# Turning every row of attention weights through DRAM, with fewer VectorE steps a row, in a two-layer graph network

## The chip, the cores and the metric

The kernel runs on one core of a Trainium2 chip. The time is the device time of one execution in microseconds (us): 2100.51 is the median of 3 runs, 2095.24 to 2102.91. The engines of the core run their own instruction queues in the order in which they were written: TensorE (PE) multiplies matrices, VectorE (DVE) and ScalarE (ACT) work on SBUF and PSUM, GpSimd (POOL) does small arithmetic, and SyncE (SP) issues nearly all DMA transfers.

## The reference, cut to what matters

There are N = 3327 nodes with 256 features each; `adj` is 3327 x 3327, sparse, with weights on its edges and on its diagonal.

```python
h = relu(layernorm(x))
# layer 0, two steps n = 0, 1, from Xf = Xa = h
R = adj + eye;  R = R / R.sum(-1)                       # row-normalised
  probs = softmax((Xa @ W1.T @ W2.T) @ (Xa @ W3.T).T)   # 3327 x 3327
  A = probs kept down from the largest until 0.9 of the sum is passed, then renormalised
  Xf = R @ Xf;  Xa = A @ Xa
  Z += Xf @ U1[n].T + Xa @ U2[n].T
x = x + layernorm(h + Z) * g + b
# layer 1, four heads of 64 on h = relu(layernorm(x))
hp = h @ W;  s = hp . a_src;  d = hp . a_dst
attn = softmax over j with adj[i, j] > 0 of leaky_relu(s_i + d_j)
x = x + elu(attn @ hp)
```

## The kernel before

All data are float32. The 3327 nodes make 26 tiles of 128 (`NT`); the last has 127.

**Layer 0** has two kinds of work. A *row* (class `Row`, one for each step and each tile i of 128 query nodes) is the whole search for the attention weights of those queries. PE computes logits in two halves (`logits`), ACT writes their exponentials into an SBUF buffer `e` of 128 x 3328 (`exps`; one row in five uses a buffer called `qq`), ACT counts and sums against trial thresholds (`count`), POOL steps the threshold (`step`, `before`), DVE picks out the largest values below it (`window`, `sort`), decides the exact cut (`choose`), and clears what lies below it (`drop`). Ties at the cut are resolved by position: the 3327 columns are cut into pieces, and each piece gets its own threshold, `thr`. The weights then have to be turned, since PE contracts over partitions. Columns 0 to 3071 are turned in three groups g of 1024 (`turn_blocks`, `put_blocks`, `get_blocks`): DVE transposes 32 x 32 blocks in place, SP writes the group to `blocks` in DRAM and reads it back with four DMAs (o = 0 to 3). Columns 3072 to 3327 are turned by PE itself (`turn`: two transposes into a PSUM tile `px`, then a copy by ACT or DVE into `et`). `BLOCKED` says which rows go this way: all 26 of step 0, the first 23 of step 1; the last three rows of step 1 are turned by PE in all 26 tiles. `attend_blocks` and `attend` multiply with `rhs`, into the PSUM bank `acca`. `finish1` and `finish2` then project a row's result; in `finish2`, `stage` and `scale` write layer 1's operand `main`.

A *full* (class `Full`, one for each step and tile t) is a block row of R @ Xf: seven loads of `adj` transposed into tiles `at` (four buffers, four j each), and 26 matmuls into the PSUM bank `accf`. The identity in R is put in afterwards: for step 0 in `take` or `add`, and in `own`, which adds c times the reciprocal sum to what is stored in `ys`.

**Layer 1** (`attend_neighbours`) goes over four blocks b of 832 query nodes, each with 26 tiles j of neighbours. SP loads adjacency tiles, ACT makes a 0/1 mask (`mask`), DVE makes the masked exponentials of four heads (`exponents`, four instructions a tile), and PE does `product` (eight matmuls, both halves c of 416 columns) and `sums` (eight, for the denominators). Sums are done for two tiles at a time (`JG = 2`). After the 26 tiles of a block `leave` copies the PSUM banks out, and `turn`, `quotient`, `parts`, `add_x1`, `join`, `store` finish seven tiles of up to 128 rows.

**The order of the work** is written by a planner (class `Plan`): every piece is given an engine, a length, a rank, the pieces that it needs, the buffers that it takes and gives back, and a lag until others see its end. The planner runs through them once and issues, on each engine, the ready piece of the lowest rank. What it writes is fixed: on the chip an engine waits at the head of its queue even if later work is ready. So a figure in the plan (a lag, a rank) moves instructions on every queue. A row's attention has rank 30n + i, its logits 2.5 less; the fulls of step 0 have min(1 + 1.15t, 27). They are what PE does when no row is ready.

Of the kernel before, what the change touches and what calls it, by code (L numbers as in the profile page):

```python
# [10 lines left out]
F32 = mybir.dt.float32  # L11
# [8 lines left out]
P = 128  # L20
# [29 lines left out]
BLOCKED = (NT, NT - 3)  # L50
# [421 lines left out]
class Plan:  # L472
# [3 lines left out]
    LAG = {"PE": 0.2, "ACT": 0.2, "DVE": 0.15, "POOL": 0.1, "SP": 2.2}  # L476
# [23 lines left out]
    def either(self, first, second, rank, *args, **kw):  # L500

        p = self.put(*first[:2], rank, first[2], *args, **kw)
        p["on"] = {e: (length, fn, self.LAG[e], 0.0) for e, length, fn in (first, second)}
        p["engine"] = ""
        return p
# [82 lines left out]
def fast(  # L588
# [58 lines left out]
    with ExitStack() as l0:  # L647
# [23 lines left out]
        blocks = spill.tile([3, 4, P, 2 * P], F32, name="blocks")  # L671
# [27 lines left out]
        def weights():  # L699
# [39 lines left out]
            a = plan.put("PE", 0.25, -200.0, turn, take=["px"], needs=[plan.put("SP", 0.02, -201.0, lambda: None, lag=8.0)])  # L739
# [126 lines left out]
        plan = Plan(dict(rows=1, mvs=3, pl=2, px=2, acca=1, accf=1, et=3, at=4, y=1, e2=3, mask=2, e5=1, qg=2, **BUFS))  # L866
# [4 lines left out]
        class Row:  # L871
# [3 lines left out]
                "b w t0 t1 t2 u g k2 p0 p1 p2 p3 D0 D1 D2 v z r0 s0 s1 s2 h x th tq mid dh kh fl d up h0 h1 room zs cnt "  # L875
# [38 lines left out]
            def exps(self, k):  # L914
                pl = self.pl.pop(k)
                to = self.e[:, PART * k : PART * k + pl.shape[1]]
                if k < 3 and self.i < BLOCKED[self.n]:
                    to = to.rearrange("p (g q t) -> p g t q", g=4, t=2)
                    pl = pl.rearrange("p (g t q) -> p g t q", g=4, t=2)
                S.activation(  # L920
                    to,
                    pl,
                    AF.Exp,
                    accum_out=(self.p0, self.p1, self.p2, self.p3)[k],
                )

            def row_sum(self):
                k = self.NAMES.index("p0")
                S.activation(self.sc[:, k + 4 : k + 8], self.sc[:, k : k + 4], AF.Copy, accum_out=self.s)
# [114 lines left out]
            def choose(self):  # L1044
# [14 lines left out]
                V.scalar_tensor_tensor(out_, win, nxt, keep, ALU.is_gt, ALU.mult, accum_out=self.cnt)  # L1059
                V.tensor_sub(self.m, met[:, 2, i], self.cnt)  # L1060
                ties = small.tile([P, PIECES * 8], F32, name="rest", bufs=1).rearrange("p (c r) -> p c r", r=8)
                V.tensor_scalar(ties, self.cands, nxt, None, ALU.is_equal)
                num, upto = (small.tile([P, 4], F32, name=name, bufs=1) for name in ("num", "upto"))
                V.tensor_reduce(num[:, :3], ties[:, :15, :].rearrange("p (a c) r -> p a (c r)", a=3), AX.X, ALU.add)
                V.tensor_reduce(num[:, 3:], ties[:, 15, :], AX.X, ALU.add)
                V.tensor_tensor_scan(upto, num, num, 0.0, ALU.add, ALU.bypass)
                V.scalar_tensor_tensor(num, upto, self.m, num, ALU.is_le, ALU.mult, accum_out=met[:, 4, i])
                self.thr = small.tile([P, 4], F32, name="thr")
                V.tensor_scalar(upto, upto, self.m, 2.0**-24, ALU.is_gt, ALU.mult)
                V.tensor_scalar(self.thr, upto, 1.0 - 2.0**-24, nxt, ALU.add, ALU.mult)  # L1070

            def drop(self, o):

                piece = self.e[:, o * PART : min((o + 1) * PART, N)]
                V.scalar_tensor_tensor(piece, piece, self.thr[:, o : o + 1], piece, ALU.is_gt, ALU.mult)  # L1075
# [6 lines left out]
            def turn(self, g):  # L1082
                m = min(4, NT - 4 * g)
                pt = self.pt[g] = ps_x.tile([P, 4, P], F32, name="px")
                for k in range(m):
                    j = 4 * g + k
                    T.transpose(pt[:, k, :], self.e[:, j * P : (j + 1) * P], ident)

            def turned_by_s(self, g):
                self.turned(g, S.copy)  # L1090

            def turned_by_v(self, g):
                self.turned(g, V.tensor_copy)

            def turned(self, g, copy):
                m = min(4, NT - 4 * g)
                self.et[g] = etpool.tile([P, 4, P], F32, name="et")
                copy(self.et[g][:, :m, :], self.pt.pop(g)[:, :m, :])

            def attend(self, g):  # L1100
                if g == 0:
                    self.acc = ps_a.tile([P, D], F32, name="acca")
                et = self.et.pop(g)
                for j in range(4 * g, min(4 * g + 4, NT)):
                    T.matmul(
                        self.acc, et[:, j - 4 * g, :], rhs[self.n][:, j, :], start=(j == 0),
                        stop=j == NT - 1 and self.i >= BLOCKED[self.n],
                    )
# [28 lines left out]
        class Full:  # L1137
# [41 lines left out]
            def add(self):  # L1179
                rs = rsum[:, self.t : self.t + 1]  # L1180
                f, here = self.f[:, :D], c[:, self.t, :]
                if not self.added:
                    V.tensor_add(f, f, self.src[:, self.t, :D])
# [934 lines left out]
```

## Time and profile before

| what | before |
|---|---|
| median of 3 runs | 2100.51 us |
| the profiled execution: its own time, its span | 2100.08 us, 2098.2 us |
| mean granted TensorE clock | 0.994 |
| layer 0 (start to 1619 us): PE, DVE, ACT, POOL busy | 1570.2, 1292.8, 1043.0, 979.6 us |
| layer 1 (1619 to 2083 us): PE, DVE, ACT busy | 463.9, 429.6, 251.2 us |
| DMA in layer 0 and layer 1 | 173 and 125 GB/s |

The profiled execution lies 0.4 us below the median. A busy time is the time in which at least one instruction of the engine was under way; matmuls overlap each other, so their mean durations are longer than the pace at which they follow one another. In the groups of PE one float32 matmul shows as two records, and a transpose as one.

### The profile page before, as it was taken

The page shows a single profiled execution, that of the slowest core. Times are in us where ns is not written, and L with a number is a line of the kernel's source. Part 1 is how long each engine was busy: PE and PEld are TensorE (multiplying, and loading weights), DVE is VectorE, ACT ScalarE, POOL GpSimd, SP SyncE. Part 2 cuts the span into 40 slices and gives each one's busy share as a digit, 9 for nine tenths or more (in the row PEclk, how much of TensorE's full clock was granted, in tenths as well). Part 3 has the DMA queues.
Part 4 walks back from the last instruction along what each step waited for, and adds up shares of the span by engine and source line. Part 5 has one row for each costly group of instructions (what it writes and reads, how often), then busy time and mean ns, then how long its engine had stood idle before and what let it go on. Part 6 is the DMA issues. An engine that isn't in the chain of part 4 may idle for free. (4 is left out here: it accounts for less than half of the span.)

```text
span 2098.2 us, 34334 instructions
## 1 busy us (share of the span) xinstructions
PE 2037.8 (97%) x10695; PEld 1415.2 (67%) x10695; DVE 1729.7 (82%) x4105; ACT 1300.0 (62%) x2480; POOL 990.7 (47%) x2170
## 2 busy tenths in 40 slices
PE   8999999999999989989999999999999999999997
PEld 6477777878787778767878787787877333333332
DVE  5689897778876871578998979988987999999895
ACT  5767665666556621777778776778652547465552
POOL 4476654446544630567778777777772000000001
PEclk9999999999999999999999999999999999999999
DMA  4188888678877685697787888887743544453341
GB/s 116 45 190 186 194 180 195 168 152 196 189 183 172 176 186 138 199 232 165 181 189 176 203 188 191 185 191 192 182 126 89 157 141 142 125 147 115 112 127 34
DMA packets 580513, 338.56 MB, mean 161 GB/s; under 512 B 327931, under 2 KB 533281, under 8 KB 580321
## 3 DMA queue, kind: packets, MB, share of 16 engines
q1 hardware_dynamic: 579424, 336.06, 66.4%
q8 instruction: 87, 1.43, 0.3%
q14 instruction: 106, 0.86, 0.1%
q10 hardware_dynamic: 896, 0.21, 0.0%
HBM read 242.86 MB, written 93.05 MB: 160 GB/s over the span
## 5 line engine op out<-in xcount | busy, mean ns | idle before, releaser
L959 ACT ACTIVATE junk<-e,sc 128x3327 fp8e5<-128x3327 f32 x147 | 451.0, 3068 | 31.4 <-POOL sc L996 29.8
L1128 PE MATMUL acca<-rhs,e 128*128 128x256 f32 x1872 | 426.8, 381 | 4.6 <-DMA e<-blocks 4.6
L1128 PEld LDWEIGHTS acca<-rhs,e 128*128 128x128 f32 x1872 | 364.9, 197 | 48.7 <-issue 6.0
L1153 PE MATMUL accf<-c,at 128*128 128x256 f32 x1352 | 316.5, 385 | 17.1 <-DMA at<-in_adjt_dram 8.5
L1153 PE MATMUL accf<-main,at 128*128 128x257 f32 x1352 | 313.3, 381 | 5.4 <-ACT main L1304 2.5
L1153 PEld LDWEIGHTS accf<-c,at 128*128 128x128 f32 x1352 | 252.8, 192 | 67.5 <-DMA at<-in_adjt_dram 10.2
L1153 PEld LDWEIGHTS accf<-main,at 128*128 128x128 f32 x1352 | 250.4, 190 | 54.3 <-issue 11.5
L1022 DVE MAX8 cands<-y 128x8 f32<-128x205 f32 (+1 forms) x832 | 242.9, 361 | 3.6
L1918 POOL TENSOR_TENSOR qq<-qq 128x256 f32<-128x256 f32 x4 | 3.0, 759 | 457.0 <-ACT qq L1914 457.0
L1017 DVE SCALAR_TENSOR_TENSOR y<-e,sc 128x1639 f32<-128x1639 f32 x84 | 165.1, 1965 | 62.9 <-POOL sc L1007 61.7
L920 ACT ACTIVATE e<-pl 128x1024 f32<-128x1024 f32 (+1 forms) x168 | 152.9, 920 | 75.4 <-PE pl L905 74.7
L1752 ACT ACTIVATE et<-at 128x448 bf16<-128x448 f32 (+1 forms) x204 | 112.6, 552 | 128.6 <-DVE e L1763 73.3
L1779 PE MATMUL pl<-e,main 128*64 128x416 f32 x1024 | 190.4, 517 | 0.1
L1075 DVE SCALAR_TENSOR_TENSOR e<-e,thr 128x1024 f32<-128x1024 f32 (+1 forms) x168 | 178.4, 1066 | 2.4 <-DMA at<-in_adjt_dram 0.3
L905 PE MATMUL pl<-kt,qg 64*128 64x512 f32 (+1 forms) x832 | 173.7, 536 | 0.4 <-ACT qq L920 0.4
L1112 DVE STREAM_TRANSPOSE e<-e 128x1024 f32<-128x1024 f32 x117 | 146.1, 1248 | 3.7
L1779 PEld LDWEIGHTS pl<-e,main 128*64 128x64 f32 x1024 | 70.3, 137 | 111.0 <-issue 91.5
L1763 DVE SCALAR_TENSOR_TENSOR e<-c,low,et 128x832 f32<-128x832 f32 x128 | 128.8, 1070 | 6.1 <-issue 3.2
L905 PEld LDWEIGHTS pl<-kt,qg 64*128 64x128 f32 x832 | 71.5, 186 | 83.4 <-issue 76.2
L1751 ACT ACTIVATE at<-at 128x448 f32<-128x448 f32 (+1 forms) x204 | 110.8, 543 | 25.7 <-DMA at<-in_adjt_dram 25.6
L1763 DVE SCALAR_TENSOR_TENSOR e<-qq,low,et 128x832 f32<-128x832 f32 x120 | 120.5, 1073 | 4.1 <-PE accf L1793 2.9
L959 ACT ACTIVATE junk<-qq,sc 128x3327 fp8e5<-128x3327 f32 x35 | 107.4, 3068 | 10.7 <-POOL sc L996 10.4
(550 smaller groups left out, 3540.7 us busy)
## 6 DMA issues: line engine op xcount, KB each, us to landing
at<-in_adjt_dram SPq DMA_DIRECT2D x414, 256.0 KB
blocks<-e SPq DMA_DIRECT2D x117, 512.0 KB
e<-blocks SPq DMA_DIRECT2D x468, 128.0 KB
at<-in_adjt_dram SPq DMA_DIRECT2D x102, 192.0 KB
blocks<-qq SPq DMA_DIRECT2D x30, 512.0 KB
qq<-blocks SPq DMA_DIRECT2D x120, 128.0 KB
at<-in_adjt_dram SPq DMA_DIRECT2D x52, 128.0 KB
ys<-ystage SPq DMA_DIRECT2D x26, 256.0 KB
```

Of the source, the lines that this page charges most:

```text
L905: T.matmul(pl[:, lo : lo + m], qg[self.n, self.i // 4][half, self.i % 4, :], kt[half, 512 * k : 512 * k + m], start=True, stop=True,)
L920: S.activation(to, pl, AF.Exp, accum_out=(self.p0, self.p1, self.p2, self.p3)[k],)
L959: S.activation(junk[:, :N], self.e[:, :N], fn, bias=t, scale=-1.0, accum_out=dst, saturate=False)
L1017: V.scalar_tensor_tensor(self.y[:, : hi - lo], self.e[:, lo:hi], self.up, self.e[:, lo:hi], ALU.is_lt, ALU.mult, accum_out=(self.h0, self. ...
L1022: V.max(self.cands[:, a * PIECES // 2 + k, :], self.y[:, at[k] - lo : at[k + 1] - lo])
L1075: V.scalar_tensor_tensor(piece, piece, self.thr[:, o : o + 1], piece, ALU.is_gt, ALU.mult)
L1112: V.transpose(part, part)
L1128: T.matmul(self.acc, lhs, rhs[self.n][:, j, :], start=(j == 0), stop=stop and j == js[-1])
L1153: T.matmul(self.acc[:, : self.w], self.at[j // JC][:, j % JC, :], self.src[:, j, : self.w], start=(j == 0), stop=(j == NT - 1),)
L1752: S.activation(to, src, AF.Sign)
L1763: V.scalar_tensor_tensor(held["e"][:, k, :], extra["both"][b % 2][:, k, :], low[:, j, k : k + 1], held["mask"], ALU.max, ALU.mult,)
L1779: T.matmul(q["acc"][a][k * FH : (k + 1) * FH, c, :C], main[:, j, h * FH : (h + 1) * FH], held["e"][:, h, c * C : (c + 1) * C], start=(j == 0),
```

## The change

It has eight parts, and the plan is made anew with all of them.

1. All rows are turned through DRAM, in all 26 tiles. `BLOCKED`, `turn`, `turned`, `attend` go. The third group now has 1280 columns: `blocks` holds 13 slices, its DVE transpose, its put and its four gets are a quarter larger.
2. `drop` has three pieces in place of four (1024, 1024, 1279 columns). `choose` finds the ties with one scan over the 128 candidates.
3. `exps` writes the last 255 columns with two instructions, of 128 and 127, into the order that the blocks want.
4. The identity is added by POOL into the diagonal tile of `at` (`diagonal`), once for each full. The additions in `take`, `add` and `own` go. PE's matmul of that tile needs the addition.
5. `stage` in `finish2` makes layer 1's operand on ACT from PSUM, with four instructions scaled by `qd`; DVE's `scale` goes.
6. In the last block of layer 1 the last six tiles (`LATE = 6`) are multiplied by halves: first half c = 0 of all six, then half c = 1. `leave_half` copies the first half out while the second is multiplied.
7. The exponentials of the first two tiles of layer 1 get rank 54.2, before the last rows of layer 0; the four `e` buffers, `c` and `rhs` are handed to layer 1 in another order (`ec`).
8. In the plan: lags of 8 in place of 6 for puts, 4 in place of 3.3 for `at` loads, 7 in place of 3 for the store to `ys`; the fulls of step 0 have rank 2 + 1.3t; empty pieces no longer take a slot of SP or POOL.

```diff
-BLOCKED = (NT, NT - 3)
-        blocks = spill.tile([3, 4, P, 2 * P], F32, name="blocks")
+        blocks = spill.tile([NT // 2, P, 2 * P], F32, name="blocks")
...
             def exps(self, k):
...
+                if k < 3:
+                    S.activation(to, pl.rearrange("p (g t q) -> p g t q", g=4, t=2), AF.Exp, accum_out=sums[k])
+                else:
+                    S.activation(to[:, 0, 0, :], pl[:, :P], AF.Exp, accum_out=self.p3)
+                    S.activation(to[:, 0, 1, : m - P], pl[:, P:], AF.Exp, accum_out=self.p4)
...
             def choose(self):
...
-                V.tensor_scalar(ties, self.cands, nxt, None, ALU.is_equal)
-                num, upto = (small.tile([P, 4], F32, name=name, bufs=1) for name in ("num", "upto"))
-                V.tensor_reduce(num[:, :3], ties[:, :15, :].rearrange("p (a c) r -> p a (c r)", a=3), AX.X, ALU.add)
-                V.tensor_reduce(num[:, 3:], ties[:, 15, :], AX.X, ALU.add)
-                V.tensor_tensor_scan(upto, num, num, 0.0, ALU.add, ALU.bypass)
-                V.scalar_tensor_tensor(num, upto, self.m, num, ALU.is_le, ALU.mult, accum_out=met[:, 4, i])
+                V.tensor_scalar(ties, self.cands.rearrange("p c r -> p (c r)"), nxt, None, ALU.is_equal)
+                V.tensor_tensor_scan(ties, ties, ties, 0.0, ALU.add, ALU.bypass)
+                self.thr = small.tile([P, PIECES], F32, name="thr")
+                V.tensor_scalar(self.thr, ties[:, 7::8], self.m, 2.0**-24, ALU.is_gt, ALU.mult)
+                V.tensor_scalar(self.thr, self.thr, 1.0 - 2.0**-24, nxt, ALU.add, ALU.mult)
+                ends = ties[:, 39:80:40]
+                V.scalar_tensor_tensor(ends, ends, self.m, ends, ALU.is_equal, ALU.mult, accum_out=met[:, 4, i])
...
+            def part(self, g):
+                return self.e[:, g * PART : (g + 1) * PART if g < 2 else NP]
...
+            def diagonal(self):
+                own = self.at[self.t // JC][:, self.t % JC, :]
+                GP.tensor_add(own, own, ident)
...
-                V.scalar_tensor_tensor(y, c[:, t, :], rsum[:, t : t + 1], y, ALU.mult, ALU.add)
-            y = plan.put("SP", 0.5, r + 0.3, store, needs=[a], give=["ystage"], lag=3.0)
+            y = plan.put("SP", 0.5, r + 0.3, store, needs=[a], give=["ystage"], lag=7.0)
...
+                for k in range(H):
+                    part = slice(k * FH, (k + 1) * FH)
+                    S.activation(main[:, t, part], pm[:, part], AF.Copy, scale=qd[:, t, k : k + 1])
...
-            if row.i < BLOCKED[row.n]:
...
-                last = plan.put("PE", 0.22, rank - 0.01, row.turn, 6, needs=[drops[3]], take=["px"])
...
+                b = plan.put("SP", 0.5, rank - 1.0, row.put_blocks, g, needs=[b], lag=8.0)
...
-                plan.put("SP", 0.4, rank, f.load, q, needs=[after], take=["at"], lag=3.3) for q in range(-(-NT // JC))
+                plan.put("SP", 0.4, rank, f.load, q, needs=[after], take=["at"], lag=4.0) for q in range(-(-NT // JC))
...
+            a, own = None, plan.put("POOL", 0.4, -90.0, f.diagonal, needs=[loads[t // JC]])
...
+                    if b == 3 and j >= NT - LATE:
+                        for c in range(2):
+                            r = rank if c == 0 else r0 + 9.0
+                            p_ = plan.put("PE", 0.71, r, product, 0, (c,), needs=[x_, last_acc, halves[c]])
+                            p_ = plan.put("PE", 0.71, r, product, 1, (c,), needs=[x_, y_, p_])
+                            halves[c] = plan.put(
+                                "PE", 0.76, r, sums, (c,), needs=[p_, last_den], give=[mine] if c else []
+                            )
+                        continue
...
+                def leave_half(c, q=q):
...
+                    for k in range(2):
+                        S.copy(q["ot"][k][:, c * C : (c + 1) * C], q["acc"][k][:, c, :C])
+                    S.copy(q["ot"][2][:, c * C : (c + 1) * C], q["den"][c][:, :C])
...
-                full(n, t, (min(1.0 + 1.15 * t, 27.0) if n == 0 else base + 1.0 + t), [p[0] for p in sources], [p[1] for p in sources] if n == 0 else loaded[0])
+                full(n, t, (2.0 + 1.3 * t if n == 0 else base + 1.0 + t), [p[0] for p in sources], [p[1] for p in sources] if n == 0 else loaded[0])
```

In the lists of instructions of the two kernels PE has 176 fewer (all transposes), DVE 337 fewer, ACT 98 more, POOL 52 more and SP 45 more; every matmul of before is still there.

## The prediction

> **What bounds the kernel now.** I read first the busy times of the page, then the same by stage, because a share over the whole span mixes two layers with different limits.
>
> ```profile
> PE 2037.8 (97%) x10695; PEld 1415.2 (67%) x10695; DVE 1729.7 (82%) x4105; ACT 1300.0 (62%) x2480; POOL 990.7 (47%) x2170
> 0.00:1619.00 1619.00, 1570.17 (x7283) 1243.54 (x7283) 1292.77 (x3596) 1042.96 (x1868) 979.59 (x2157) 0.99 0.74 173
> 1619.00:2083.00 464.00, 463.91 (x3392) 169.52 (x3391) 429.59 (x488) 251.16 (x597) 5.53 (x6) 1.00 0.43 125
> 2083.00:2098.00 15.00, 3.73 (x25) 2.18 (x21) 7.37 (x21) 5.92 (x16) 5.59 (x7) 0.72 0.20 64
> ```
>
> The columns of the last three lines are the stretch, its length, the busy time of PE, PE's weight loads, DVE, ACT and POOL, the granted clock, the DMA share and GB/s. In layer 0 PE is idle for 1619.0 - 1570.2 = 48.8 us, in layer 1 for none, and after it comes a tail of 15 us. So the time is PE's work, plus 48.8, plus the tail. DVE, at 1292.8 of 1619, has no claim of its own except through latency.
>
> A busy PE need not be at its best pace, so next I read how closely its instructions follow one another, in the order of time.
>
> ```profile
> 1567.91 1.04 PE L1087 MATMUL px<-ident,e 128*128 128x128 f32 x8
> 1568.78 1.89 PE L1105 MATMUL acca<-rhs,et 128*128 128x256 f32 x8
> 1570.51 0.60 PE L1087 MATMUL px<-ident,e 128*128 128x128 f32 x4
> ...
> 2065.94 5.81 PE L1779 MATMUL pl<-e,main 128*64 128x416 f32 x32
> 2071.68 0.91 PE L1793 MATMUL acca<-e,qd 128*32 128x416 f32 x8
> ...
> 2074.61 0.57 PE L1779 MATMUL pl<-e,main 128*64 128x416 f32 x2
> ```
>
> Each line begins with start and length. Eight transposes take 1568.78 - 1567.91 = 0.87 us until the next work starts, 0.109 each; four attention matmuls take 1.73, 0.4325 each. In layer 1 two tiles j take 2074.61 - 2065.94 = 8.67 us. The groups give the number of transposes that go (156 on `e`, 20 on `qq`) and the fulls' and attention's waits:
>
> ```profile
> L1128 PE MATMUL acca<-rhs,e 128*128 128x256 f32 x1872 | 426.8, 381 | 4.6 <-DMA e<-blocks 4.6
> L1153 PE MATMUL accf<-c,at 128*128 128x256 f32 x1352 | 316.5, 385 | 17.1 <-DMA at<-in_adjt_dram 8.5 <-ACT main L1164 5.4 <-DVE main L1167 3.1
> L1087 PE MATMUL px<-ident,e 128*128 128x128 f32 x156 | 27.7, 286 | 8.5 <-ACT ystage L1347 8.5
> L1087 PE MATMUL px<-ident,qq 128*128 128x128 f32 x20 | 4.0, 281 | 0.0
> ```
>
> Last I looked for the two largest holes in PE:
>
> ```profile
> 750.99 0.59 ACT L1347 COPY ystage<-px 128x512 f32<-128x512 f32 x1 [9.55 <-DMA ys<-ystage]
> 751.63 0.69 PE L1087 MATMUL px<-ident,e 128*128 128x128 f32 x2 [7.18 <-ACT ystage L1347]
> 752.11 3.25 PE L1128 MATMUL acca<-rhs,e 128*128 128x256 f32 x8
> ...
> 907.24 5.99 PE L1153 MATMUL accf<-c,at 128*128 128x256 f32 x16 [6.18 <-DMA at<-in_adjt_dram]
> ```
>
> In the first, a row's two transposes stood at the head of PE's queue and waited for a `px` tile, which `stage` held because its own buffer was still being stored to `ys`. The four matmuls after it took 3.25 us, not 1.89: the granted clock of that slice is 0.83. The hole cost 7.2 + 1.4 = 8.6 us. The second is a late `at` load, behind seven gets on SP.
>
> **The change, part by part.** The sum is made against the profiled 2100.1 us, 0.4 below the median.
>
> *Transposes (part 1).* 49 rows x 2 and 3 x 26 are 176. PE does nothing else while it issues them: 176 x 0.109 = -19.2 us. Their busy time, 31.7, counts overlapping ends and is the largest gain; the smallest is 0, if PE then waits for rows (a rival). The matmuls stay, at the 0.38 us mean of both groups. What is late next: a row's last columns now come back from DRAM. In a row of step 1 the first put was issued at 1228.6 and its attention began at 1245.3, so a row is ready some 17 us after its first group is turned. For the last row, whose clearing began at 1591.0, PE had 26 matmuls of fulls left, 11.2 us, and now the first products of two tiles, 5.6 (the product part of a pair, below): cover for 17 us. I take 0; without the cover it costs up to 17.
>
> By the Trainium skill (VectorE: DVE Perf Modes, The three transpose paths and the rules after it) VectorE turns only 32 x 32 blocks, a full 128 x 128 belongs to TensorE, and a strided plain DMA copy is far slower than the crossbar's; it speaks against this change. If that rule set the price, the 19.2 would not be gained. The row shows that PE is what is short, so the sum keeps it.
>
> *More DMA (part 1).* Puts were 147 x 512 KB; now 104 x 512 + 52 x 640, 11.5 MB more, and as much read back: 23 MB on 280 MB in layer 0 (173 GB/s x 1619 us), 8%. Slices of 20 us reached 251 GB/s, so there is room, but SP issues a get in 0.5 us at the median and eight in 7.2 us when the queues are full, and `at` loads stand behind them. PE's waits on `at` and blocks are 8.5 + 1.9 + 4.6 = 15 us. Bounds: 0, and these doubled, 15. I take +1, 8% of them, as the load grows by that.
>
> The Trainium skill (DMA: Bandwidth & Descriptors, Specifications) asks for pieces of 512 B or more for line rate; the gets move 256 B. If the added reads ran at half of 251 GB/s, my estimate is 92 + 46 us of transfer time, still spread beside 1619 us, so the sum would not change by it.
>
> *Three drops, new `choose`, no `take`, `own` and `scale` (2, 4, 5).* All DVE. Removed: PSUM copies 12.6, `own` 12.6, additions 10.8, 3.9 and `scale` 16.2, and 0.13 a row in `drop` (4.26 to 4.13, the 1279 columns at the pace of 1024 in 1.27). Added: 0.31 a row in `turn_blocks`, three more rows of 4.06, 5.7 for copies that the plan moves from ACT. `choose` loses 1.57 of small steps and gains 0.81 and a scan over 128, between 0.26 (a scan over 32) and four times that. Together 16 to 56 us less of 1293. ACT gains about 35 (four scaled copies of 0.215 for one of 0.369; one more exponential and its read) and loses 18.7 of copies, beside 576 us of idle time. Neither sets the end: 0. If PE were not the bound, DVE's part would be worth up to 56.
>
> *Identity on POOL (4).* 52 additions, each half of the 0.757 of a 256-wide one: 20 us of POOL, which idles for 639 in layer 0. But POOL must now wait for a load, with the row's `before` and `step` behind it, and after these ACT's count and DVE's window; and PE's matmul waits for POOL. Before, there is no such wait of PE. Bounds: 0, and 52 x 0.38 = 20 if PE paid every one. I take +2, since only one matmul in 26 is concerned and a load is ahead by up to four buffers.
>
> *The `ys` lag and `px` (8).* The first hole: 0 to -8.6. Its transposes are gone, but other users of `px` can still meet the same store: -6.
>
> *Halves at the end (6).* A half of a tile is eight of the 32 product records and eight of the 32 sum records above, but product and sum now alternate 12 times, not 3. In the trace weight loads of a product follow at 0.349 for two records and sums at 0.70 for eight, so the pair of 8.67 us is 5.58 + 2.79 of pace and 0.30 for two changes; a half is 1.40 + 0.70 + 0.30 = 2.40, twelve are 28.8, against 26.0. The tail: three of seven tiles are turned and divided beside the second half (their transposes, 1.65, and 0.6 of changes come before PE's end); after it come copies and first transposes, 1.4, then four tiles at ACT's 0.8. Last join at about 6.4 us after PE's end, before 8.35. Sum 2.8 + 2.25 - 1.95 = +3. Bounds: -2 (the alternation free) and +5.
>
> *Early exponentials, ranks (7, 8).* PE has no hole between 1581 and 2083, and DVE four times 1.0 against PE's 4.33 a tile: 0.
>
> Sum: -19.2 + 1 + 2 - 6 + 3 = -19.2, so 2081 us.
>
> **The rivals.** *The rows set the pace.* If the search chain, not PE, decides when step 1 ends, the 19.2 turns into waits: 2100. For it: DVE is at 549.5 of 620 between 920 and 1540, and 48.8 us of holes exist. Against: PE is at 607.3 there, and fulls are always at hand.
>
> *Slower: `at` loads come late.* Mechanism: the larger gets hold SP, as before 907. One such hole costs 6.2 + 2.4 (16 records in 5.99, elsewhere 3.62) = 8.6. It decides from four more holes; at five, one in ten rows, 2081 + 43 = 2124. Against: only one hole of that kind in 52 rows.
>
> *More gain.* The plan's new lags close holes. Without the 9.4 of the first 100 us and the first hole, 30.8 remain; half of them and the whole first hole: 2081 - 15.4 - 2.6 = 2063.
>
> *It doesn't do what it says:* coarser tie pieces could send the run into the fallback `general`, far outside the range.
>
> **How the numbers follow.** The sum's case, 2066 to 2090, 0.58; more gain, 0.15; rows set the pace, 2090 to 2111, 0.14; late loads, 0.12; fallback, 0.01. Within 0.5%, some 10 us, this kernel's measurement tells nothing from no change. Faster 0.73, same 0.14, slower 0.13. The range 2056 to 2108 leaves out about 0.05 below and 0.12 above.
>
> **What would show it.** Right: no transposes on `e`; PE busy about 1551 before layer 1 and idle under 45; no hole behind `ys`; a last block about 3 us longer in PE, a tail 2 shorter; POOL hardly ever named as what PE waited for. Wrong: PE idle grown by 19, ended by DMA of blocks (rows), of `at` (late loads), or by POOL.

## The result, and the profile after

The changed kernel takes 2112.4 us (median of 4 runs, 2110.2 to 2114.1) against 2099.7 us of the kernel before (4 runs beside it): 1.0061 of its time, 95% interval 1.0040 to 1.0082, so slower by some 0.6%. In a later set of runs on one chip it took 2110.0 us, 1.0045 (1.0028 to 1.0062). Below, "after" is taken as 2111.2, the mean of the two medians; the kernel before had medians of 2099.5 to 2101.3 in all sets. The prediction was 2081, so it was wrong in sign and by 30 us.

These are the busy times of the page of the kernel after, and the stretches of layer 0 (to the first sums), layer 1 and the tail, with the columns of the prediction's first fence.

```profile
PE 2033.4 (96%) x10519; PEld 1398.5 (66%) x10519; DVE 1693.6 (80%) x3768; ACT 1297.6 (61%) x2630; POOL 1028.4 (49%) x2222
0.00:1632.80 1632.80, 1567.06 (x7143) 1231.14 (x7146) 1265.98 (x3271) 1049.15 (x2030) 1017.10 (x2210) 0.99 0.83 187
1632.80:2098.10 465.30, 464.29 (x3369) 166.19 (x3369) 422.91 (x485) 244.97 (x592) 8.15 (x8) 0.99 0.41 118
2098.10:2110.30 12.20, 2.08 (x16) 1.19 (x12) 4.71 (x12) 3.51 (x9) 3.15 (x4) 0.69 0.16 46
```

In the kernel before, the first sums start at 1623.4 us, with PE busy for 1574.6 of it, and from there to the end are 474.8 us. So layer 0 is 9.4 longer, and layer 1 with its tail 2.7 (477.5). In layer 0 PE's idle time grew from 48.8 to 65.7 us, although 176 transposes are gone, and PE's busy time there fell by 7.5 only. DMA is at 187 GB/s in place of 173 there, and over the whole kernel it moved 361.6 MB in place of 338.6.

The groups of PE that the prediction showed of the kernel before now read:

```profile
L1098 PE MATMUL acca<-rhs,e 128*128 128x256 f32 x2184 | 489.6, 381 | 18.1 <-DMA e<-blocks 7.0 <-DVE win L1036 2.7 <-DVE e L1070 2.6
L1123 PE MATMUL accf<-c,at 128*128 128x256 f32 x1352 | 311.8, 385 | 17.4 <-DMA at<-in_adjt_dram 9.0 <-ACT main L1137 5.6 <-POOL at L1130 2.2
```

The idle time ahead of the rows' attention (the figure behind the last bar) was 4.6 and is 18.1 us; behind it stand many different releasers, the largest with 7.0. (The 8.5 us ahead of the transposes is gone with them.) Summed over all of PE's waits up to the first sums, by the engine that ended them, the waits for DVE grew from 3.5 to 16.7 us and those for loads of `adj` and of blocks from 15.1 to 23.9, while those for ACT fell from 26.5 to 19.4. Where the time went shows in slices of 20 us at the end of layer 0 of the kernel after:

```profile
1480.00:1500.00 20.00, 16.82 (x76) 13.43 (x77) 17.27 (x52) 13.41 (x28) 11.48 (x26) 1.00 1.11 223
1500.00:1520.00 20.00, 17.12 (x74) 14.11 (x73) 12.94 (x23) 12.96 (x25) 15.25 (x31) 0.91 0.60 159
1520.00:1540.00 20.00, 19.21 (x91) 16.85 (x90) 17.17 (x45) 12.24 (x26) 15.37 (x32) 1.00 0.92 201
1540.00:1560.00 20.00, 16.25 (x68) 13.49 (x67) 14.28 (x45) 10.14 (x15) 13.69 (x31) 0.91 1.19 232
1560.00:1580.00 20.00, 17.85 (x77) 14.38 (x75) 18.10 (x31) 7.25 (x8) 16.22 (x30) 0.91 0.85 260
1580.00:1600.00 20.00, 18.16 (x83) 14.86 (x80) 19.16 (x46) 3.03 (x11) 6.97 (x8) 1.00 0.85 151
1600.00:1620.00 20.00, 18.23 (x87) 12.84 (x86) 13.76 (x30) 5.36 (x10) 5.33 (x7) 1.00 1.12 225
```

PE (second number) is idle for 1 to 4 us in each of them, the DMA share (last but one) is 0.60 to 1.19, and the granted clock falls to 0.91 in three. In the kernel before, the slices from 1580 to 1620 were full at a DMA share of 0.25 to 0.32:

```profile
1580.00:1600.00 20.00, 20.00 (x107) 16.57 (x107) 19.27 (x51) 5.45 (x12) 6.50 (x10) 1.00 0.32 93
1600.00:1620.00 20.00, 20.00 (x97) 16.91 (x97) 7.12 (x26) 3.94 (x10) 2.41 (x6) 1.00 0.25 74
```

From 1480 us to the first sums PE idles 20.4 us (152.8 - 132.4) where it idled 5.9 (143.4 - 137.5). Before 1480 it idles only 2.5 more: 4.2 more at the change of steps (680 to 860 us), less elsewhere.

What the last row waited for is seen in SP's queue, ACT's and PE's at that place:

```profile
1593.57 0.39 SPq L1086 DMA_DIRECT2D blocks<-e  x1
1598.32 2.05 SPq L1117 DMA_DIRECT2D at<-in_adjt_dram  x2
1600.47 0.39 SPq L1086 DMA_DIRECT2D blocks<-e  x1
...
1603.50 0.38 SPq L1678 DMA_DIRECT2D at<-in_adjt_dram  x1
1603.97 0.46 SPq L1086 DMA_DIRECT2D blocks<-e  x1
...
1614.04 3.62 SPq L1091 DMA_DIRECT2D e<-blocks  x4
```

```profile
1630.19 0.63 ACT L1688 ACTIVATE at<-at 128x512 f32<-128x512 f32 x1 [4.21 <-DMA at<-in_adjt_dram]
...
1632.25 0.46 ACT L1102 ACTIVATE xa<-acca,sc 128x256 f32<-128x256 f32 x1
```

```profile
1622.72 4.48 PE L1098 MATMUL acca<-rhs,e 128*128 128x256 f32 x20
1627.13 1.62 PE L1716 MATMUL pl<-e,main 128*64 128x416 f32 x8
1632.76 1.62 PE L1730 MATMUL acca<-e,qd 128*32 128x416 f32 x8 [4.01 <-ACT xa L1102]
```

VectorE had turned the last row's second and third group at 1595.8 and 1599.1; their puts (L1086) went out at 1600.5 and 1604.0, 4.6 and 4.9 us later, behind `at` loads, which wait for a buffer to come free (from PE, and those of layer 1, L1678, from ACT). The last gets went out at 1614.0, and the last matmuls began at 1622.7. These ended at 1627.1, but ACT's `attended` (L1102) stood behind a `mask` of layer 1 (L1688) that waited 4.2 us for its load, and so PE stood still for 4.0 us. These links are instructions that were ready and stood behind one that was not. From the last row's first put (1593.6) to the end of layer 0 PE is idle for 5.8 us; the rest of the 20.4 lies before, from 1480 us on.

Two other readings bear on the terms of the sum. The hole behind `ys` at 751 us is gone. And the last block with its halves:

```profile
2066.79 1.62 PE L1716 MATMUL pl<-rhs,main 128*64 128x416 f32 x8
2068.34 0.90 PE L1730 MATMUL acca<-rhs,qd 128*32 128x416 f32 x8
2069.18 1.62 PE L1716 MATMUL pl<-e,main 128*64 128x416 f32 x8
...
2083.02 0.92 PE L1716 MATMUL pl<-rhs,main 128*64 128x416 f32 x4 [1.01 <-ACT y L1801]
```

A half takes 2.39 us (2069.18 - 2066.79), as estimated (2.40); at the change of halves there is a wait of 1.0 for `leave_half`, which was not in the sum. The tail is 12.2 us, from 14.9.

### The profile page after: what moved, and what is told of

It is laid out like the page before. It is cut to its first block, busy times and chain, and to the rows that moved or that the text cites. A ratio compares the mean times of both kernels' runs of the same rounds, so it can differ in the third digit from the quotient of the medians.

```text
span 2110.3 us, 33982 instructions
## 1 busy us (share of the span) xinstructions
PE 2033.4 (96%) x10519; PEld 1398.5 (66%) x10519; DVE 1693.6 (80%) x3768; ACT 1297.6 (61%) x2630; POOL 1028.4 (49%) x2222
## 5 line engine op out<-in xcount | busy, mean ns | idle before, releaser
L1098 PE MATMUL acca<-rhs,e 128*128 128x256 f32 x2184 | 489.6, 381 | 18.1 <-DMA e<-blocks 7.0
L1098 PEld LDWEIGHTS acca<-rhs,e 128*128 128x128 f32 x2184 | 425.6, 197 | 70.3 <-issue 13.8
L1123 PE MATMUL accf<-main,at 128*128 128x257 f32 x1352 | 322.2, 387 | 13.0 <-DMA at<-in_adjt_dram 6.7
L1123 PE MATMUL accf<-c,at 128*128 128x256 f32 x1352 | 311.8, 385 | 17.4 <-DMA at<-in_adjt_dram 9.0
L919 ACT ACTIVATE e<-pl 128x1024 f32<-128x1024 f32 x126 | 137.6, 1099 | 65.7 <-PE pl L904 64.1
L1082 DVE STREAM_TRANSPOSE e<-e 128x1024 f32<-128x1024 f32 (+1 forms) x126 | 168.6, 1338 | 7.1 <-POOL sc L993 0.5
L1070 DVE SCALAR_TENSOR_TENSOR e<-e,thr 128x1024 f32<-128x1024 f32 (+1 forms) x126 | 171.0, 1357 | 1.5 <-issue 0.4
L1688 ACT ACTIVATE at<-at 128x448 f32<-128x448 f32 (+1 forms) x204 | 110.6, 542 | 45.3 <-DMA at<-in_adjt_dram 44.0
L1700 DVE SCALAR_TENSOR_TENSOR e<-qq,low,et 128x832 f32<-128x832 f32 x120 | 121.8, 1077 | 10.6 <-ACT et L1689 3.8
L1102 ACT ACTIVATE xa<-acca,sc 128x256 f32<-128x256 f32 x52 | 24.2, 466 | 158.3 <-PE acca L1098 158.3
```

The lines of the kernel that those rows point to most:

```text
L919: S.activation(to, pl.rearrange("p (g t q) -> p g t q", g=4, t=2), AF.Exp, accum_out=sums[k])
L1070: V.scalar_tensor_tensor(piece, piece, self.thr[:, at : at + 1], piece, ALU.is_gt, ALU.mult)
L1082: V.transpose(part, part)
L1098: T.matmul(self.acc, lhs, rhs[self.n][:, j, :], start=(j == 0), stop=(j == NT - 1))
L1123: T.matmul(self.acc[:, : self.w], self.at[j // JC][:, j % JC, :], self.src[:, j, : self.w], start=(j == 0), stop=(j == NT - 1),)
L1700: V.scalar_tensor_tensor(held["e"][:, k, :], extra["both"][b % 2][:, k, :], low[:, j, k : k + 1], held["mask"], ALU.max, ALU.mult,)
```

## The experiments

Times are medians; the ratio is to the kernel before, with its 95% interval.

**The last three rows by PE.**

```diff
-            (every row through DRAM)
+            BLOCKED = (NT, NT - 3): the last three rows of step 1 keep plain column order in exps,
+            and take turn, turned_by_s or turned_by_v, and attend for all 26 tiles, as before
```

> The kernel after, with the last three rows of step 1 turned by PE again (72 transposes more, at 0.127 us about +9). Theory C (the cover at the end is gone): of the 19.6 us that PE idles between 1480 us and the first sums of layer 1 at least 13 go, and some 4 of lost clock: 13 + 4 - 9 = 8 faster, about 2104 us. Theory S (the loss is spread over layer 0, in the new order of the work and the heavier DMA queues): nothing is won at the end and the transposes are paid, about 2120 us.

Measured: 2104.5 us, 1.0019 (1.0004 to 1.0034), so theory C's number. The first sums come at 1625.3 in place of 1632.8. The slice 1600 to 1620, of this kernel, is full again with little DMA:

```profile
1600.00:1620.00 20.00, 20.00 (x98) 17.53 (x97) 8.56 (x27) 4.21 (x13) 2.59 (x6) 1.00 0.22 63
```

From 1480 us to the first sums PE now idles 10.6 us, not 20.4. So the last three rows cost idle time at the end, but that is not the whole loss: this kernel has 98 transposes fewer than before and is still not faster. It also moves 10.2 MB less by DMA than the kernel after (351.4 MB), so this run does not part the lost cover from the traffic. (The last three rows bring back 78 transposes, not the 72 of the expectation.)

**LATE = 0.**

```diff
-            LATE = 6
+            LATE = 0
```

> The kernel after, with LATE = 0: the last block of layer 1 as in the kernel before. If the halves cost +3 as the prediction had it, 2109 us; if the +5.4 us of layer 1 in the trace are the halves and only the tail of -2.7 stands against it, 2110 us; if the +5.4 is mostly the lowered clock after the hole at 1629 to 1633 us and the halves win their tail, 2114 us.

Measured: 2109.6 us, 1.0036 (1.0022 to 1.0049). From the first sums to the end it takes 474.0 us in place of 477.5: the halves cost 3.5, close to the +3 of the prediction.

**The old figures of the plan.**

```diff
-  lag=8.0 (puts), 4.0 (at loads), 7.0 (ys);  2.0 + 1.3 * t
+  lag=6.0 (puts), 3.3 (at loads), 3.0 (ys);  min(1.0 + 1.15 * t, 27.0)
```

> The kernel after, with the plan's figures of the kernel before (lags 6, 3.3 and 3, fulls of step 0 at rank min(1 + 1.15t, 27)). If the figures made the loss (rows of step 0 run up to 47 us ahead, and step 0's fulls are then waited for at the change of steps: 12.8 us of holes and 5 of clock between 700 and 800 us, against 8.6 and 3.4 before), about 2102 us, the rows no longer ahead, and holes near 750 us like before. If the loss is the cover at the end, 2108 to 2116 us with the holes after 1480 us as they are. If the figures help, as the prediction took them to (-6), 2118 us.

Measured: 2183.6 us, 1.0397 (1.0366 to 1.0428); none of the three, and the direction is that of the third. With the fulls early the rows come late, and at the end no full is left to fill PE's queue while the last rows are searched. The last row of step 0 is through at 829 us (773 in the kernel after), the last full at 1649 and the last row at 1706. The time line of PE in this kernel:

```profile
1644.84 4.48 PE L1123 MATMUL accf<-c,at 128*128 128x256 f32 x20
1670.33 2.05 PE L1098 MATMUL acca<-rhs,e 128*128 128x256 f32 x4 [21.01 <-DVE rest L1038]
```

**Without the early exponentials.**

```diff
-  rank = r0 + 9.0 * j / NT if b > 0 or j >= 2 else 54.2 + 0.1 * j
+  rank = r0 + 9.0 * j / NT
```

> The kernel after, without the early exponentials (the first two tiles of layer 1 at their old rank). Theory E (they stand in VectorE's queue ahead of the last row: 2.1 + 2.1 us between 1570 and 1582 us, within its search): the last row is cleared about 4 us earlier, 2108 us. Rival (they give PE the first products as filler, 7.6 us, in the holes at the end): those holes grow, 2116 to 2120 us.

Measured: 2110.4 us, 1.0046 (1.0030 to 1.0061), not to be told from the kernel after. Neither theory holds; part 7 is worth about nothing.

**The added columns not moved.** The expectation speaks of 23 MB; the run takes away 13.6 of them (361.6 to 348.0 MB), since the last three rows still go through DRAM.

```diff
-  src = self.part(g)...;  to = self.part(g)[...]
+  src = self.part(g)[:, :PART]...;  to = self.part(g)[:, :PART][...]
+  i = j if j < 24 else j - 2      # weights of tile i for tile j
```

> The kernel after, with the added DMA left out and the order of all instructions as it was: put and gets of the third group move 1024 columns again, and the matmuls of tiles 24 and 25 take tiles 22 and 23 as weights, so the weights of the last 256 columns are not used (a wrong result), and the fallback is never taken. If the added 23 MB cost what the prediction said, +1, 2111 us. Theory D (heavier queues slow everything: blocks and adjacency tiles land later, PE's and POOL's waits on them grow): back by 10, 2102 us, with POOL's 45 us of waits for in_x and PE's 15.7 + 8.2 for tiles and blocks towards the 15 and 10.5 + 4.6 of before.

Measured: 2089.2 us, 0.9943 (0.9926 to 0.9960). All instructions stand in the same order as in the kernel after, no DMA fewer is issued, and 13.6 MB less make it 22 us faster. This is the term that the prediction put at +1 and bounded by 15. Of the waits that theory D named, POOL's for `in_x` went from 45.1 to 26.0; PE's own did not change, in the kernel after and then in this one (total, times, longest):

```profile
PE accf L1123 <- DMA at<-in_adjt_dram: 15.7, 8, 3.8
PE acca L1098 <- DMA e<-blocks: 7.0, 11, 1.5
```

```profile
PE accf L1124 <- DMA at<-in_adjt_dram: 15.7, 10, 4.1
PE acca L1099 <- DMA e<-blocks: 7.2, 7, 1.9
```

PE's idle time in layer 0 falls all the same, from 65.7 to 51.8 us: its waits for DVE go from 16.7 to 4.8 and those for ACT from 19.4 to 13.9.

**Without POOL's identity.**

```diff
   def diagonal(self):
-      GP.tensor_add(own, own, ident)
+      pass                            # and add() takes 1 + the row sum
```

> The kernel after, with POOL's 52 additions of the identity left out (R lacks the identity, its row sums keep the 1; a wrong result), and the fallback never taken; the order of everything else stays. By the prediction's +2, 2110 us; by the waits that PE shows on it (2.8 us, and up to 4 of POOL's queue behind), 2107 us. Theory P (POOL's 40 us of waiting for tiles holds up the search's steps and the ystage additions behind it, and so the rows): 2100 us or below.

Measured: 2115.6 us, 1.0063 (1.0037 to 1.0089): no faster than after. POOL's 40 us of waits for the tile, and PE's 2.8 for POOL, cost nothing that can be measured; theory P falls for this load.

**The kernel before without its transposes.**

```diff
   def turn(self, g):
+      if self.i < BLOCKED[self.n]: return
   (turned copies from e; attend(6) takes tiles 0 and 1 of e as weights)
```

> The kernel before, with the 98 transposes of the rows that go through DRAM left out and nothing put in their place: the order is the same, the copy to et copies other numbers, the matmuls of tiles 24 and 25 take tiles 0 and 1 as weights (a wrong result), and the fallback is never taken. It is the price of the transposes by itself. By the prediction (0.109 each) -10.7, and the hole of 8.6 at 751 us goes with the px wait: 2081 us. Rival Z (they stood in gaps that PE has anyway, in waits for weights or blocks): only the hole goes or is found again one instruction later, 2092 to 2100 us.

Measured: 2083.8 us, 0.9923 (0.9901 to 0.9946), 16 faster, not quite 19. The stretch with the first hole, 680 to 860 us, in the kernel before and then in this one:

```profile
680.00:860.00 180.00, 170.14 (x782) 139.88 (x779) 100.88 (x303) 71.20 (x130) 59.74 (x127) 0.98 0.71 168
```

```profile
680.00:860.00 180.00, 177.46 (x818) 144.97 (x818) 105.72 (x314) 74.23 (x130) 64.85 (x142) 1.00 0.74 178
```

PE idles 2.5 us there, not 9.9, at full clock: the hole of 8.6 went with the `px` wait. The first sums come 15.6 earlier (1607.8), so 7.0 remain for 98 transposes, 0.07 each; the second hole, near 900 us, came out some 2 longer here with its clock, so up to 0.09.

**The last rows by PE and LATE = 0** (the first two diffs together).

> The kernel after with two parts undone at once: the last three rows of step 1 by PE, and LATE = 0. If the cover at the end (-8) and the halves (-3 to -5) are separate things, 2100 us, as fast as the kernel before; if both were the same hole at the start of layer 1, 2104 us.

Measured: 2099.8 us, 0.9992 (0.9978 to 1.0006), as expected of two separate things: 9.8 less than with LATE = 0 alone, 4.8 less than with the last rows alone.

**Part 1 alone undone.** The last two tiles of every row go by PE again, and the last three rows wholly; parts 2 to 8 stay. (The last two tiles are multiplied at the end of a row here; in the kernel before they came ahead of the last eight.)

```diff
-  part(g): e[:, g * PART : (g + 1) * PART if g < 2 else NP]
+  part(g): e[:, g * PART : (g + 1) * PART]
+  last = plan.put("PE", 0.22, rank - 0.01, row.turn, 6, needs=[drops[2]], take=["px"])
+  last = plan.either(ACT or DVE: turned to et);  attend(6) at the end of the row
+  BLOCKED = (NT, NT - 3), as in the first run
```

> The kernel after with part 1 alone undone: columns 3072 to 3327 are turned by PE (104 transposes in 49 rows and the 78 of the last three), the third group has 1024 columns, 23 MB less by DMA; all other parts as they are. If part 1 is the whole loss: 2112 - 23 (the added columns through DRAM) - some 8 (the last rows) + 11 to 13 (98 transposes and the px tile that they wait for) gives 2088 to 2094 us, faster than the kernel before. If the other parts lose too (figures, POOL's identity, halves), and the 23 was luck of that one order, 2104 us or more.

Measured: 2076.7 us, 0.9883 (0.9867 to 0.9900). That is 11 under the lowest figure expected. Part 1 is the whole loss, 34 us; the rest of the change gains 24. (The transposes in the 49 rows are 98, not the 104 of the expectation.)

**Parts 1 and 6 undone.**

> The same with LATE = 0: the kernel after with parts 1 and 6 undone. By the -3 to -5 that LATE = 0 has shown twice, 2086 to 2090 us, the fastest of all; if the halves only lost because layer 1 began in a hole, as the one above.

Measured: 2072.4 us, 0.9863 (0.9847 to 0.9880): the fastest version, 28 us under the kernel before and 39 under the kernel after, and again well under the figure expected; LATE = 0 itself gave 4.3, within its -3 to -5. Its layer 0, in the columns of the first fence:

```profile
0.00:1595.80 1595.80, 1568.61 (x7311) 1243.06 (x7312) 1248.46 (x3291) 1059.20 (x2057) 1017.53 (x2212) 1.00 0.75 176
```

PE idles 27.2 us there, where it idled 48.8 before and 65.7 after; the clock loses 1.8 us, before 8.6, after 11.0 ((1 - clock) x 20, summed over slices; this counts a low clock while PE stands idle, too).

**The columns written but not read back** (the diff of the run without the added columns, for the gets alone).

> The kernel after, with the added columns written to DRAM but not read back (the gets move 1024 columns, the matmuls of tiles 24 and 25 take tiles 22 and 23 as weights, a wrong result; the fallback is never taken). Put and gets together were worth 23 us, in 6.8 MB each, but the write has pieces of 1 KB and the reads pieces of 256 B. If the small pieces cost, nearly all 23 go with the gets: 2092 us. If bytes cost, half: 2101 us. If it is the longer put that the row waits for, 2108 us or more.

Measured: 2097.5 us, 0.9984 (0.9972 to 0.9996). From after, the gets are worth 13.7 and the puts 8.3 (2097.5 - 2089.2), for 6.8 MB each: between "bytes" and "small pieces". Each of the two figures is uncertain by some 4 to 5 us, so their difference does not tell the cases apart.

**The kernel after itself.**

> The kernel after itself, beside the others on the same chip: 2112 us, 1.006 of the kernel before.

Measured: 2110.0 us, 1.0045 (1.0028 to 1.0062).

**Part 1 undone, without its transposes** (the diff of the kernel before without its transposes, on top).

> The kernel with part 1 undone (2077 us), with its 98 transposes left out and nothing in their place (the order as it was; the matmuls of tiles 24 and 25 take tiles 0 and 1 as weights, a wrong result; the fallback is never taken). It is the gross gain that part 1 was to bring, in the order without holes. At the 0.09 to 0.11 us that a transpose took in the kernel before: 2066 to 2068 us. If they stand in gaps that PE has anyway: 2074 us or more, and then part 1 had nothing to win.

Measured: 2070.1 us, 0.9845 (0.9826 to 0.9863). The 98 transposes cost 6.7 us, 0.07 each, in an order with few holes; that lies between the two figures expected. The two runs' intervals leave some 5 us of doubt on it (0.02 to 0.12 each), so 0.109 is not excluded, and the trace of the kernel with part 1 undone still shows that pace for a pair:

```profile
165.04 0.38 PE L1088 MATMUL px<-ident,qq 128*128 128x128 f32 x2
165.26 1.03 PE L1157 MATMUL accf<-main,at 128*128 128x257 f32 x4
```

The work behind the pair starts 0.22 us after the pair does, 0.11 for each transpose; that is also the median over this trace's pairs.

**No added DMA, in the order of after** (last rows by PE, added columns not moved).

> The kernel after with the last three rows of step 1 by PE, and the added columns not moved by DMA (as in the run that left put and gets out): no transposes in 49 rows and no added DMA, so the same matmuls and the same traffic as in the run above, in the order that the plan of the kernel after gives. If the cost of part 1 is the traffic, it comes near the run above: 2066 to 2072 us. If 21 for the added columns and 8 for the last rows are all that the traffic costs, 2084 us, and the 16 us between this and the run above are the order of the plan (a row's last ten tiles wait for its last gets, where before the two last tiles could go ahead).

Measured: 2081.7 us, 0.9921 (0.9897 to 0.9945). By 1480 us the two read

```profile
0.00:1480.00 1480.00, 1451.43 (x6645) 1142.76 (x6646) 1161.59 (x3079) 1001.43 (x1944) 949.95 (x2082) 1.00 0.77 179
```

```profile
0.00:1480.00 1480.00, 1445.60 (x6615) 1137.03 (x6616) 1161.11 (x3036) 989.41 (x1913) 944.66 (x2075) 1.00 0.78 179
```

with the same traffic and 5.8 us more of idle PE in the second. The 2081.7 is nearer to the second figure expected. The 11.6 us between the medians (5.2 between the two profiled executions) are the plan's order, and with it VectorE's transpose of 1280 columns in place of 1024, which this run does not separate.

**Parts 1 and 6 undone, with the old figures.**

> The kernel with parts 1 and 6 undone (2072 us), with the plan's figures of the kernel before (part 8 undone but for the empty pieces). With the kernel after, the old figures cost 71 us. If the figures are where the other parts win: 2095 us or more. If the old figures only fit badly with rows that come late through DRAM, and the win is in the work that VectorE no longer does and in the ys hole: 2072 to 2080 us.

Measured: 2129.0 us, 1.0139 (1.0122 to 1.0157). The figures are where the other parts win: 57 us here, 71 in the kernel after. With the old figures the other parts are 28 us slower than the kernel before, so the new figures and the rest of the change win only together.

**Without the loads of x.**

```diff
   def fetch():
-      nc.sync.dma_start(xr, x[t * P : (t + 1) * P, :])
   def add_b():
-      GP.tensor_add(held["xr"], held["xr"], late["b"])
+      GP.tensor_copy(held["xr"], late["b"])
```

> The kernel after, with the 26 loads of x in the second half of layer 0 (3.4 MB) left out, and POOL's addition to them made a copy (the residual x is left out, a wrong result; the fallback is never taken). In the kernel after POOL's queue waits 45 us for these loads, up to 10.7 at a time, with the steps of the search behind it; in the fastest kernel 7 us. Theory Q (the traffic costs through POOL's queue: rows come late because their steps stand behind these waits): 10 to 20 us faster, 2092 to 2102 us. Rival (rows have slack for it, or the cost is spread over all loads): by 3.4 of 13.6 MB of the traffic's 22 us, about 5 us, 2105 to 2111 us.

Measured: 2100.0 us, 1.0002 (0.9991 to 1.0014): 11 faster with 3.4 MB less, at the lower end of theory Q and twice its share of bytes. These are POOL's waits for loads in the kernel after, and in the fastest one (total, times, longest):

```profile
POOL ystage L1374 <- DMA ystage<-in_x_dram: 45.1, 14, 10.7
POOL at L1130 <- DMA at<-in_adjt_dram: 40.5, 20, 4.9
```

```profile
POOL at L1164 <- DMA at<-in_adjt_dram: 24.3, 12, 4.5
POOL ystage L1408 <- DMA ystage<-in_x_dram: 7.4, 5, 2.8
```

This points to POOL's queue as one of the paths, through the loads of x, with the search's steps behind them. It is not shown: the run also takes 26 loads out of SP's queue, and the 11 and the 5 of the rival differ by little more than the intervals allow.

**The wide write in the fastest kernel.**

```diff
-  src = self.part(g)...
+  src = self.e[:, g * PART : (g + 1) * PART if g < 2 else NP]...
```

> The kernel with parts 1 and 6 undone (2072 us), with the third group's write to DRAM 1280 columns wide, as in the kernel after, where nothing reads the added part (6.8 MB more; the result stays right). In the kernel after, that write alone cost 2097 - 2089 = 8 us. If traffic costs the same in any order: 2080 us. If it costs only where loads are late already: 2072 to 2076 us.

Measured: 2075.4 us, 0.9883 (0.9864 to 0.9902): 3 more, not 8, as the second case had it. With some 5 us of doubt on either figure, this suggests and does not show that the price of the same traffic depends on how much is late already.

**The fastest kernel without early exponentials.**

> The kernel with parts 1 and 6 undone, and the early exponentials of part 7 at their old rank. In the kernel after that gave 2 to 3 us: 2069 us. If it only helped rows that came late through DRAM: 2072 us; if the early products are filler before layer 1: 2076 us.

Measured: 2074.1 us, 0.9887 (0.9867 to 0.9907): no gain, so the 2 to 3 us of the earlier run are not confirmed.

## Why the prediction was wrong, step by step

The kernel before was read rightly: PE is what is short, and its idle time and the clock behind its holes decide. The sum failed in part 1, and a second failure of the other sign hid nearly half of it: part 1 was put at -18 (-19.2 + 1 + 0) and measured at +34.5; the other parts were put at -1 (+2 - 6 + 3) and measured at -24. That the two misses differ in sign is luck; without part 1 the same sum would have been too high. Part 1 as measured, from run to run:

| step | from | us |
|---|---|---|
| 98 transposes gone | 2076.7 to 2070.1 | -6.7 |
| the plan's new order, and the longer transpose on VectorE | 2070.1 to 2081.7 | +11.6 |
| added columns written and read, 49 rows | 2081.7 to 2104.5 | +22.9 |
| the last three rows through DRAM, without their 78 transposes | 2104.5 to 2111.2 | +6.7 |
| sum | 2076.7 to 2111.2 | +34.5 |

Each line has an uncertainty of some 5 to 6 us (the intervals of its two runs, added as squares); the third was also measured in the kernel after itself (22.0), and the fourth beside LATE = 0 (9.8).

- *Transposes, -19.2.* The mechanism was right. 98 of them cost 6.7 to 9 us, 0.07 to 0.09 each, where 0.109 gives 10.7; with some 5 us of doubt, that the price was too high is not shown. The other 78 were not measured by themselves. The bounds held.
- *What is late next, taken as 0.* This step failed. The 17 us of latency were those of a row in the middle of step 1, and only the last row was asked about. For that row the comparison nearly held: 19.8 us from its first put (1593.6) to its attention (1613.4), with the puts 4.6 and 4.9 us behind `at` loads on SP, and PE idle for 5.8 in all, 4.0 of it because `attended` stood behind a mask on ACT. The larger part of the idle time at the end lies ahead of it, while the rows before it are at work. All three rows together cost 7 to 10 net, their 10.2 MB of traffic included; with the 5 to 8 that 78 transposes are worth, 12 to 18, about the 17 that the prediction named for no cover at all.
- *More DMA, +1, bounded by 15.* This step failed most, and it turned the sign: 22 to 23 for the added columns, outside the bounds. The bound doubled PE's own waits on loads, 15 us. But PE's waits on adjacency tiles are the same (15.7) with and without the 13.6 MB, and those on blocks too; what traffic delays is the work of other engines, which PE meets as waits for DVE and ACT (together 36.1 us with it, 18.7 without). By which queue it gets there (SP's puts behind loads, POOL's steps behind the loads of x) is argued from the time lines and not shown run by run. "There is room" was read from the highest rate of a slice, 251 GB/s, which says nothing of the queue ahead of one transfer.
- *The new order.* The 11.6 us (some 6 of doubt) were in no term: the sum treated the plan as given and only took the transposes out of it.
- *Identity on POOL, +2.* Nothing measurable (2115.6 without it).
- *The `ys` lag and `px`, -6; ranks, 0.* The other parts together gained 24 us (2100.5 to 2076.7), 28 without part 6. The -6 and the 0 failed too, the other way. The mechanism of the rival "more gain" is real: idle time fell to 27.2 us and the lost clock to 1.8. The prediction had given it 0.15 and tied it to the whole change. (Its 30.8 us of remaining holes took the 1.4 us of slow matmuls off the idle time as well; 32.2 remain.) That the figures matter so much here (57 to 71 us) is shown; why they suit this kernel and not the one before is only argued: before, `own` in `finish1` held a `ystage` buffer until the full of the same tile was done, so fulls had to come early; with the identity already in `at`, they may come late, and serve as filler. The new figures were not tried in the kernel before.
- *Halves, +3.* 3.5 in layer 1's length, 1.6 to 4.8 in medians: right, with a wait of 1.0 that was not foreseen. *Early exponentials, 0*: right. *DVE and ACT, 0*: VectorE has 44 us less to do in the kernel with part 1 undone (1686.1 against 1729.7), within the 16 to 56 estimated; what that is worth by itself was not tried.
- *The rivals.* "Rows set the pace" came nearest (idle grown by 17, where it named 19), with a reason that held in part: PE waited 16.7 us for DVE where it had waited 3.5, but VectorE was not busy to its limit, its share fell from 82% to 80%, and waits for blocks grew by 4 us only. "Late `at` loads" named the right resource and the wrong victim. PE's waits on them rose only from 10.5 to 15.7, not by four holes.

On the rule weighed in the prediction: the Trainium skill (VectorE: DVE Perf Modes, Rules for kernel authors) gives a full 128 x 128 transpose to TensorE, if PSUM will do as its target. The runs side with it: undoing part 1 is worth 34 us. The prediction set the rule aside because PE is short; PE is short, and 98 transposes on it, some 7 us, are still cheaper than the way through DRAM. The piece size of 512 B or more that the Trainium skill (DMA: Bandwidth & Descriptors, Specifications) asks for does not set the price: the 1 KB writes, which keep the rule, cost 8.3 us too, and that the 256 B reads cost more (13.7) is not clear of the noise.

## What to carry to other kernels

To price traffic, take the bytes away and leave every instruction where it is. A mean DMA share of 0.83 was not room here: an engine works its queue in order, so a late transfer becomes a wait of whatever stands behind it. Ask of every engine's queue what stands behind a load, not only of the engine that is short. And undo the parts of a many-part change one by one: here one part of eight cost 34 us and hid a gain of 24. Undo the figures of a planner with them: the same parts under the old figures lost 28.

## What the runs showed of the hardware that was not expected

- 13.6 MB more, 4% of the traffic, cost 22 us, 1% of the time, with every instruction in its place. 6.8 MB of writes cost 8 us there and 3 us in the fastest kernel, each with some 5 us of doubt.
- A float32 transpose of 128 x 128 on PE holds up the work behind it for 0.11 us, in a pair (0.22 us) as in a run of eight (0.87), though it shows a duration of 0.28 us in the groups. Leaving out 98 of them gave 6.7 to 9 us.
- Short holes can cost clock too. The slice 1500 to 1520 of the kernel after has one hole of 2.9 us and a clock of 0.91, which takes 1.8 us more (0.09 x 20); the line is below. In the fastest kernel the slice 960 to 980 has the same clock after a hole of 2.4 us. The Trainium skill (TensorE: Matmul & The Clock Gate, Why this matters for your kernels) asks for no gaps over about 3 us; here two below it counted.

```profile
1508.37 12.31 PE L1123 MATMUL accf<-c,at 128*128 128x256 f32 x48 [2.88 <-ACT main L1137]
```
